# Decoder stack: the first two row tiles of the expert stage prepared inside the gated attention

## The chip, the cores and the metric

The kernel runs on one core of a Trainium2 chip. The metric is the device time of one execution in microseconds (us): the median over runs of the same program. A profile is one further execution, recorded instruction by instruction, with a time of its own. The engines are named as in the profile: PE is TensorE (PEld its weight loads), DVE VectorE, ACT ScalarE, POOL GpSimd, SP SyncE, which only issues DMAs here.

## The reference

The input x has 16 blocks of 128 tokens with 512 features, in f32. Six sublayers follow each other, each as `x = layernorm(x + sublayer(x))`: a state-space scan, a cross attention, a ternary feed-forward, a self attention, a gated cross attention, and a mixture of experts. The change touches the last two.

Gated attention (16 heads of 32), per batch of 128 tokens against 128 context tokens: `out = softmax(q k^T) v @ wo.T`, then `sigmoid(x @ wg.T) * out`, where x is the RMS-normed input.

Experts: a router scores 64 experts and keeps the 8 best; the 64 lie in 8 groups of 8. For each group g a token has `scalar` (the sum of its kept weights in that group) and `soft` (the softmax over the kept ones):

```python
xg = x[:, None, :] + jnp.einsum('ngi,ghi->ngh', soft, mask_up_w)
g = jnp.einsum('ngh,gih->ngi', xg, gate_proj_w)
u = jnp.einsum('ngh,gih->ngi', xg, up_proj_w)
d = jnp.einsum('ngi,ghi->ngh', silu(g) * u, down_proj_w)
y = jnp.einsum('ng,ngh->nh', scalar, d)
```

A group in which a token has nothing (scalar 0) adds nothing for it, so only the tokens of a group need be computed.

## The kernel before, in words

The stages run in the order of the sublayers: scan, cross attention, feed-forward, then `stage_attention`, which holds both the self attention (8 pairs of blocks) and the gated attention (8 pairs), and `stage_moe`. The x blocks stay in SBUF throughout.

**Gated attention.** `stage_attention` has a list `units` of 16 pairs x 8 = 128 entries, and a loop over steps t from -2 to 129. In step t, unit t gets its exponentials on ACT (`exps`, L1184), unit t-1 its row sums and scaling (`norm`: DVE L1190 and L1191, POOL L1192), unit t-2 its transpose on TensorE (`pts`, copied to `at_T` by ACT L1028 or DVE L1030; the PSUM tile of it has one buffer). Side jobs are Python generators in a list `running`; each gets one `next` per step. `project` makes q and the gates of a pair ahead of its units; `values`, started when half a pair is turned, multiplies with v (`ao`), copies (`oT`), multiplies with wo (`pw`, L1214), gates on DVE (L1217) and adds to x on POOL (L1218), and after the second half normalises the pair. After the loop, a `while running` drains what is left. The last pair's attention ends with a `pw`, a gate and an add.

**Routing.** From step 84 on, an object `Moe` lives in `k.moe`. Its `setup` loads the router, the weights of expert group 0 (`first`) and, by `prepare`, the mask table `mup[0]`. `tick` runs `route` for a pair of finished blocks: it transposes x, scores, chooses, and forms rows of 776 numbers per token: 512 of x, 4 x 64 of group softmax (a high and a low part), 8 of `scalar`. `scatter` writes each row to DRAM (`rows`), and by indirect DMA on POOL's queue (L1492) to the next free place in `bucket[half][g]` of every group that the token uses. Blocks 0 to 7 are the first half, and are routed while the gated attention works on blocks 8 to 15; blocks 8 to 15 are routed from step 3 of the expert loop on.

**Experts.** `stage_moe` walks `units` of (half, group, tile): 128 rows each, 6 tiles for a bucket of 768 rows, 8 for the last group of the second half, 98 in all. It is a software pipeline over steps t, in which a unit passes through
- `fetch` (L1502, SP): 128 rows, 388 KB, from the bucket into tile `row`, 6 buffers, 5 steps ahead;
- `places` (L1507, L1509), 3 ahead: TensorE turns the 128 softmax columns (`pts`), ACT copies them to `soft`;
- `masks` (L1513, L1515), 2 ahead: TensorE multiplies with `mup` (`pm`), DVE adds x (`xg`);
- `turn_in` (L375, L1521), 1 ahead: four transposes (`ptx`), copied by ACT to `xgT`;
- `gate_up` (L1529 to L1533): 4 chunks of `pg` and `pu`, each recorded as two matmuls, Silu on ACT, product with `scalar` on DVE into `act`; `pg` and `pu` have one PSUM buffer each;
- `turn_act` (L1539), `down` (L1546, `y`), `store` (L1556, and a DMA on ACT's queue), one and two steps later.

`load` fetches the 2.1 MB of weights of the next group on SP, `prepare` casts its mask table (ACT L1368, three DVE operations), `combine` gathers results by indirect DMA on POOL's queue and adds them to x there.

**Memory.** Pools are opened and closed like a stack, from two sides. The attention's work pool `s4w` is on the left; the router's `s6r`, in `k.moe_ctx`, is on the right and stays to the end. When `stage_attention` returns, its pools close, and `stage_moe` opens `s6w` (row, soft, xg, xgT, act and so on), `s6m` (weights) and `s6u` (mask tables) in their place. In PSUM the attention has `s4p` (tag `pp`, two buffers), `s4s`, `s4t`, `s4o`; the experts have `s6g` (pg, pu), `s6p` (tag `pp`, three buffers), `s6k` (pm), `s6y`.

**Order.** The language's framework places the waits and orders the instructions of each engine by itself: the order in which the program writes them is their rank, and one of lower rank goes ahead where its own estimate of durations says that the one of higher rank isn't ready. Each engine then works its queue in that order. So the order of the trace isn't always that of the program: `turn_in` of unit 1 is written ahead of `gate_up` of unit 0, and stands behind its first two pairs in the trace.

## Time and profile before

| | us |
|---|---|
| median of 3 runs | 3377.56 (3376.58 to 3380.5) |
| profiled execution | 3382.4 |
| its span, first to last instruction | 3380.6 |
| PE busy | 3153.0 (93%) |
| DVE, POOL, ACT busy | 1876.7, 1389.5, 1379.5 |
| last matmul of the attention (pw) starts, group lasts | 2480.81, 3.70 |
| first matmul of the experts (pts) starts | 2489.80 |
| first gate_up matmul (pg) starts | 2494.01 |
| last y group starts, lasts | 3364.12, 5.32 |

The expert stage thus takes about the last 890 us of the span. The profile tells, for each stretch of time, how long each engine was busy and at which granted clock TensorE ran (1.00 is full); for each instruction, its start, its duration, and in square brackets how long its engine was idle before it and what ended that; and for each wait, its engine and line, what it waited for, the total, how often and the longest. In the timeline, neighbouring instructions of a kind are merged (x8), and matmuls overlap, so starts are to be compared with starts. A group of `pg` and `pu` matmuls that runs freely starts every 0.59 us for two of them; the ends of matmuls are modelled.

### The profile page before, as it was taken

To read this page: it belongs to the slowest core of one execution; us is meant where nothing else is said; L and a number is where in the kernel's file an instruction comes from. 1 tells how busy PE (TensorE), PEld (TensorE's weight loads), DVE (VectorE), ACT (ScalarE), POOL (GpSimd) and SP (SyncE) were. 2 spreads that over 40 slices of the span, in tenths; PEclk is the share of its full clock that TensorE was granted. 3 is DMA by queue.
4 is the path that set the end of the run, shared out by engine and by line. 5 is a ranking of instruction groups with operands and counts; after the bars stand their busy time and mean duration, and the time that the engine had idled before them with its cause. 6 is when DMAs were issued, how large, how long until landed. Compare 5 with 4: busy or idle time off the path is not lost. (4 is left out here: it accounts for less than half of the span.)

```text
span 3380.6 us, 38522 instructions
## 1 busy us (share of the span) xinstructions
PE 3153.0 (93%) x12894; PEld 1813.6 (54%) x12944; DVE 1876.7 (56%) x4202; ACT 1379.5 (41%) x3299; POOL 1389.5 (41%) x1198
## 2 busy tenths in 40 slices
PE   6888999899999999999799989998989999989998
PEld 3444444355555555555466555665655566556665
DVE  5877888456556556455576669765643232222223
ACT  4655655133333233234333379865643232112221
POOL 6967887133323333332000066325624454233331
PEclk8999999899999999999899989999999999999999
DMA  6887332200000000002200010013335665445441
GB/s 230 261 259 223 98 88 69 68 7 4 7 4 4 7 4 4 7 1 94 91 1 1 17 47 1 11 57 148 137 133 175 201 233 189 163 156 172 163 158 65
DMA packets 161553, 317.28 MB, mean 94 GB/s; under 512 B 19113, under 2 KB 82089, under 8 KB 158276
## 3 DMA queue, kind: packets, MB, share of 16 engines
q1 hardware_dynamic: 123012, 215.83, 20.8%
q0 software_dynamic: 19328, 64.56, 5.5%
q10 hardware_dynamic: 19008, 34.35, 2.7%
q8 instruction: 105, 1.72, 0.2%
q14 instruction: 100, 0.82, 0.1%
HBM read 238.80 MB, written 129.04 MB: 109 GB/s over the span
## 5 line engine op out<-in xcount | busy, mean ns | idle before, releaser
L245 POOL TENSOR_TENSOR dBx<-dtx,BC 128x1024 f32<-128x1024 f32 x128 | 301.2, 2373 | 44.8 <-DVE h L258 35.1
L1529 PE MATMUL pg<-gu,xgT 128*128 128x352 f32 x784 | 301.7, 467 | 0.0
L1529 PE MATMUL pu<-gu,xgT 128*128 128x352 f32 x784 | 299.6, 464 | 0.0
L1546 PE MATMUL y<-dn,aT 128*128 128x512 f32 x588 | 268.3, 592 | 0.0
L1533 DVE SCALAR_TENSOR_TENSOR act<-pu,row,act 128x352 f32<-128x352 f32 x98 | 57.1, 583 | 376.3 <-PE pu L1529 317.9
L575 POOL TENSOR_TENSOR pr<-pr,sm 128x512 f32<-128x512 f32 x128 | 134.7, 1053 | 289.6 <-DVE sm L574 244.2
L236 ACT ACTIVATE h<-dt,negA 128x254 f32<-128x254 f32 x512 | 239.8, 474 | 14.9 <-DVE dt L178 2.1
L1572 POOL TENSOR_TENSOR x<-got,x 128x512 f32<-128x512 f32 x120 | 152.2, 1274 | 226.4 <-DMA got<-results,gidx 225.2
L606 PE MATMUL po<-w,aT 128*128 128x512 f32 x512 | 232.2, 597 | 1.1 <-DVE aT L600 1.1
L483 PE MATMUL pq<-w,xT 128*128 128x512 f32 x512 | 228.9, 594 | 0.0
L1565 POOL DMA_INDIRECT got<-results,gidx x120 | 116.2, 968 | 268.9 <-DMA results<-yo 216.1
L460 POOL TENSOR_TENSOR m<-m,m 128x512 f32<-128x512 f32 x96 | 121.6, 1267 | 247.0 <-DVE m L455 247.0
L258 DVE TENSOR_TENSOR_SCAN h<-h,dBx 128x1024 f32<-128x1024 f32 x80 | 183.0, 2294 | 71.0 <-ACT h L236 48.7
L568 ACT ACTIVATE pr<-sc,mx,sf 128x256 f32<-128x256 f32 x256 | 142.8, 562 | 187.0 <-DVE mx L561 176.1
L267 PE MATMUL py<-hC,ident 128*128 128x512 f32 x320 | 164.6, 643 | 49.1 <-ACT y L272 49.1
L1529 PEld LDWEIGHTS pu<-gu,xgT 128*128 128x128 f32 x784 | 151.2, 193 | 85.1 <-issue 4.2
L1529 PEld LDWEIGHTS pg<-gu,xgT 128*128 128x128 f32 x784 | 144.1, 194 | 64.7 <-issue 3.0
L1532 ACT ACTIVATE act<-pg 128x352 f32<-128x352 f32 x98 | 45.5, 464 | 318.6 <-PE pg L1529 248.9
L1546 PEld LDWEIGHTS y<-dn,aT 128*128 128x128 f32 x588 | 104.1, 190 | 100.8 <-issue 94.2
L1521 ACT COPY xgT<-ptx 128x512 f32<-128x512 f32 x98 | 57.5, 587 | 233.9 <-PE ptx L375 209.6
L483 PEld LDWEIGHTS pq<-w,xT 128*128 128x128 f32 x512 | 93.5, 190 | 102.0 <-issue 99.0
L606 PEld LDWEIGHTS po<-w,aT 128*128 128x128 f32 x512 | 95.4, 191 | 96.9 <-issue 92.9
(363 smaller groups left out, 6808.3 us busy)
## 6 DMA issues: line engine op xcount, KB each, us to landing
bucket<-zeros SPq DMA_DIRECT2D x96, 388.0 KB
row<-bucket SPq DMA_DIRECT2D x90, 388.0 KB
BC<-bcd SPq DMA_DIRECT2D x128, 256.0 KB
results<-yo ACTq DMA_DIRECT2D x90, 256.0 KB
gu<-in_moe_guT SPq DMA_DIRECT2D x16, 1408.0 KB
cT<-in_ctxT SPq DMA_DIRECT2D x32, 256.0 KB
dn<-in_moe_downT SPq DMA_DIRECT2D x16, 512.0 KB
rows<-r_row SPq DMA_DIRECT2D x16, 388.0 KB
```

What stands on the lines that cost most here:

```text
L236: nc.scalar.activation(h[:, c, :, 1:], st.dt[:, c].rearrange("p (b t) -> p b t", b=BQ)[:, :, 1:], AF.Exp, scale=negA[:, c, n : n + 1])
L245: nc.gpsimd.tensor_tensor(dBx, st.dtx, BC[:, 0].unsqueeze(1).to_broadcast([P, KC, TQ]), ALU.mult)
L258: nc.vector.tensor_tensor_scan(hf, hf, df, 0.0, ALU.mult, ALU.add)
L267: nc.tensor.matmul(st.py[c], k.ident, st.hC[n][:, 2 * c : 2 * c + 2], start=n == 0, stop=n == NS - 1)
L460: nc.gpsimd.tensor_tensor(m1, m1, m2, ALU.add)
L483: nc.tensor.matmul(ps, src[:, c], w[c], start=c == 0, stop=c == KC - 1)
L568: nc.scalar.activation(pr[:, j], st.sc[g, i][:, j], AF.Exp, scale=st.sf[:, h : h + 1], bias=st.mx[g, i][:, j : j + 1], accum_out=sm[:, j : ...
L575: nc.gpsimd.tensor_tensor(pr, pr, sm.unsqueeze(2).to_broadcast([P, 2, 2 * P]), ALU.mult)
L606: nc.tensor.matmul(st.po, aT[:, j], k.wo[h // 8][:, h % 8], start=h == 0, stop=h == G * J - 1)
L1529: nc.tensor.matmul(ps, u.xT[:, c], gu[:, c, lo : lo + I], start=c == 0, stop=c == KC - 1)
L1546: self.nc.tensor.matmul(u.y, u.aT[:, c], u.w[1][:, c], start=c == 0, stop=c == 2)
L1572: nc.gpsimd.tensor_tensor(k.x[b], got, k.x[b], ALU.add)
```

## The change

A new generator `open` makes a small pool `s6o` on the right side, in `k.moe_ctx`, and there the tiles row, soft, xg and xgT of two units, which are the first two tiles of `bucket[0][0]`. It is put into `running` at step len(units)-8 = 120 of the attention's loop, so its first step runs in step 121: the two row DMAs. Two steps later it does `places` for the first and the second unit, then `masks` for each, then `turn_in` for each, one per step. `masks` takes its PSUM tile from the attention's `pp` buffers there. `stage_moe` uses these two units for its first two, leaves out their fetch, places, masks and turn_in, and starts its loop at t = -3 in place of -5. Everything else of the two units (`act` and after) still lives in `s6w`, as do the rows of units 2 and up. The pool of 15.4 KB per partition stays open to the end.

```diff
@@ -1286,6 +1286,9 @@
             if k.moe:
                 k.moe.tick()
                 k.moe.send()
+            if t == len(units) - 8:
+                assert not (k.moe.now or k.moe.sending or k.to_route)
+                running.append(k.moe.open())
         while running:
             k.moe.tick()
             for job in list(running):
@@ -1498,8 +1501,24 @@
 
 
     def fetch(self, u):
-        u.row = self.wk.tile([P, self.ROW], F32, tag="row", name="row", bufs=6)
+        u.row = self.wk.tile([P, self.ROW], F32, tag="row", name="row", bufs=self.depth)
         self.nc.sync.dma_start(u.row, u.src)
+
+    def open(self):
+
+        self.wk = self.k.moe_ctx.enter_context(self.k.tc.tile_pool(name="s6o", bufs=2, side="right"))
+        self.pm, self.depth, self.opened = self.pp, 2, []
+        for j in range(2):
+            u = Ctx()
+            u.g, u.src = 0, self.k.bucket[0][0][j * P : (j + 1) * P, :]
+            self.opened.append(u)
+            self.fetch(u)
+        yield
+        yield
+        for link in (self.places, self.masks, self.turn_in):
+            for u in self.opened:
+                link(u)
+                yield
 
     def places(self, u):
         at = D + P * (u.g // 4)
@@ -1509,7 +1528,7 @@
         self.nc.scalar.copy(u.soft, pt)
 
     def masks(self, u):
-        pm = self.pm.tile([P, D], F32, tag="pm", name="pm")
+        pm = self.pm.tile([P, D], F32, tag="pp" if self.pm is self.pp else "pm", name="pm")
         self.nc.tensor.matmul(pm, u.soft, self.mup[u.g], start=True, stop=True)
         u.xg = self.wk.tile([P, D], F32, tag="xg", name="xg")
         self.nc.vector.tensor_tensor(u.xg, pm, u.row[:, 0:D], ALU.add)
@@ -1588,7 +1607,7 @@
     nc, tc, m = k.nc, k.tc, k.moe
     NG, T, H = m.NG, m.TILES, NB // 2
     with ExitStack() as ctx:
-        m.wk = wk = ctx.enter_context(tc.tile_pool(name="s6w", bufs=2))
+        m.wk, m.depth = ctx.enter_context(tc.tile_pool(name="s6w", bufs=2)), 6
         wp = ctx.enter_context(tc.tile_pool(name="s6m", bufs=2))
         mp = ctx.enter_context(tc.tile_pool(name="s6u", bufs=1))
         m.pgu = ctx.enter_context(tc.tile_pool(name="s6g", bufs=1, space=PSUM))
@@ -1600,7 +1619,7 @@
             for g in range(NG):
                 last = h and g == NG - 1
                 for j in range(H if last else T):
-                    u = Ctx()
+                    u = Ctx() if len(units) >= len(m.opened) else m.opened[len(units)]
                     u.h, u.g, u.j, u.b = h, g, j, H + j
                     u.src, u.to = (k.rows[u.b][:, :], None) if last else (
                         k.bucket[h][g][j * P : (j + 1) * P, :], k.results[h][g][1 + j * P : 1 + (j + 1) * P, :]
@@ -1613,7 +1632,7 @@
                 if next(job, running) is running:
                     running.remove(job)
 
-        for t in range(-5, len(units) + 4):
+        for t in range(-3, len(units) + 4):
             if t == 3:
                 k.to_route += range(H // 2, H)
             m.tick()
@@ -1626,6 +1645,8 @@
                 if not 0 <= t - lag < len(units):
                     continue
                 u = units[t - lag]
+                if u in m.opened and what in (m.fetch, m.places, m.masks, m.turn_in):
+                    continue
                 if what == m.fetch:
                     u.w = None
                 if what == m.gate_up:
```

## The prediction

> **What bounds the kernel now.** I read the page's engine totals and slices first (TensorE 93% busy, 9 tenths in almost every slice of the expert stage), then stretches of 15 us around the hand-over from attention to experts, then the waits of TensorE there, then the order of single instructions. Stretches (columns: bounds, length, busy time and count of PE, PEld, DVE, ACT, POOL; granted clock; DMA share; GB/s):

> ```profile
> 2455.00:2470.00 15.00, 14.14 (x105) 8.16 (x104) 9.05 (x25) 13.60 (x55) 7.51 (x7) 1.00 0.01 2
> 2470.00:2485.00 15.00, 11.58 (x96) 5.94 (x96) 7.94 (x25) 3.91 (x12) 4.58 (x4) 1.00 0.01 1
> 2485.00:2500.00 15.00, 9.20 (x25) 5.74 (x26) 5.29 (x18) 3.25 (x6) 1.26 (x1) 0.66 0.84 281
> 2500.00:2515.00 15.00, 15.00 (x62) 9.78 (x61) 5.48 (x9) 4.58 (x11) 0.00 (x0) 1.00 0.73 249
> ```

> TensorE is full before 2470 and after 2500; in between it is partly empty, and from 2485 to 2500 what it does runs at a clock of 0.66. The waits of TensorE (2440 to 2520) name the cause, and its timeline gives the places:

> ```profile
> PE pts L1507 <- DMA row<-bucket: 5.3, 1, 5.3
> PE ao L1204 <- ACT at_T L1028: 0.7, 1, 0.7
> PE pw L1214 <- ACT oT L1210: 0.7, 1, 0.7
> ```

> ```profile
> 2480.81 3.70 PE L1214 MATMUL pw<-x_wo,oT 128*128 128x512 f32 x8 [0.70 <-ACT oT L1210]
> 2489.80 0.45 PE L1507 MATMUL pts<-ident,row 128*128 128x128 f32 x1 [5.29 <-DMA row<-bucket]
> 2490.64 0.79 PE L1513 MATMUL pm<-mup,soft 128*128 128x512 f32 x1 [0.40 <-ACT soft L1509]
> ...
> 2494.01 1.54 PE L1529 MATMUL pg<-gu,xgT 128*128 128x352 f32 x2
> 2495.35 1.38 PE L1529 MATMUL pu<-gu,xgT 128*128 128x352 f32 x2
> 2496.52 1.06 PE L375 MATMUL ptx<-ident,xg 128*128 128x128 f32 x4
> ...
> 2506.87 0.49 PE L1539 MATMUL pta<-ident,act 128*128 128x128 f32 x3
> ```

> The last attention product ends at 2484.51. The first expert product starts at 2494.01, behind a DMA, a transpose, the mask product and a second transpose. Why the DMA is so late is told by SyncE and GpSimd:

> ```profile
> 2432.98 0.32 SPq L1099 DMA_DIRECT2D v<-x_v  x1
> 2486.61 1.27 SPq L1502 DMA_DIRECT2D row<-bucket  x3
> 2487.92 0.43 SPq L1381 DMA_DIRECT2D gu<-in_moe_guT  x1
> ```

> ```profile
> 2485.32 1.26 POOL L1218 TENSOR_TENSOR x<-x,gate 128x512 f32<-128x512 f32 x1 [5.65 <-DVE gate L1217]
> ```

> SyncE had nothing to do for 53 us; the rows go out 0.03 us after the last reader of attention's work pool (2485.32+1.26 = 2486.58). It is the room, not the data, that holds them. Call this release R.

> **What the stretch is worth.** My mark is 2506.87, where gate_up of units 0 and 1 is done. From 2484.51 to it are 22.36 us. At the full clock the work in it is: gate_up twice, 16 matmuls at the 0.296 us spacing of the timeline after 2504 = 4.73 each, 9.46; 4 pts at 0.11, 3 pm at 0.32, 3 ptx at 0.44 (from start to the next start, after 2504); together 12.2. So 10.2 us are lost: 5.29 waiting for the row, 0.97 for soft and xg, some 3.9 to the low clock and the act handshake (pg and pu have one buffer each).

> **The change, part by part.** Moved, for each of two units: one 388 KB row DMA on SyncE, one pts (0.11) and its soft copy (ACT 0.27), one pm (0.32) and its add (DVE 0.69), four ptx matmuls (0.44 together) and the xgT copy (ACT 0.59). In all: two DMAs, TensorE 1.74 us, ACT 1.72, DVE 1.38; nothing on GpSimd.

> The two DMAs. SyncE's queue is empty from 2433.3 to 2486.6, so nothing stands behind them. They need the last scatter into the first bucket, issued at 2430.09 by GpSimd; an indirect transfer elsewhere in the trace is used 3.7 us after issue (got, 2520.47, added at 2524.15). Landed well before 2450, and places comes at step 123, near 2459. Cost nothing; were they held until 2459, a landing of 3.2 us (2486.61 to 2489.80) would hold TensorE in attention for that long.

> The tail of attention. ACT is 13.60 of 15 us busy until the last exponentials (2471.5), then nearly idle. DVE has no gap from 2471.56 to 2478.3, where it carries a layernorm and two at_T copies for which pts waits. TensorE idles 0.86+1.41+0.73+0.70 = 3.70 us between 2469 and 2481. If all moved work falls into idle time, the tail grows by nothing; if none does, by TensorE's 1.74. An add of 0.69 that lands in DVE's full stretch is late at at_T, then at the last ao and pw. I take 1.0, a little over half.

> What it opens. Once xgT of unit 1 is copied, gate_up(0) has its inputs. pg and pu lie in s6g, which is opened first as s4p was, so I take its room as free when the last s4p tile is read, which is that copy. No row shows this. Early end: gate_up(0) puts 1.43 us into the gaps at 2479 and 2480.8 and finishes 3.30 us after the last pw, at 2487.8. Late end: it starts at R, ends at 2491.3. In both, act(0) needs the new pool and so R, a Silu of 0.46 and a DVE multiply of 0.58: gate_up(1) starts 0.6 us later, loses another 0.7 on pu, and takes 4.73. Then pts, pm and ptx of unit 2 and a pts of unit 3 add 0.98. The mark is at 2487.8+0.6+0.7+4.73+0.98 = 2494.8 early, 2498.3 late; with the 1.0 of the tail 2495.8 and 2499.3. Saved: 11.1 or 7.6. I take the early end, since the pool that is replaced is read no later than that.

> Rows 2 and 3. Row 2 is now first at R and lands at 2489.8 plus the tail, while gate_up(0) and (1) cover it. Before row 3 stand row 2, gu and dn: 388+1408+768+388 = 2952 KB at the 346 GB/s of 2488 to 2500 is 8.5 us from 2487.5, 2496 to 2497. It is needed for gate_up(3), about 2506: covered, if its pts is not queued ahead of gate_up(1).

> The mask table of expert 1 and the following ones are cast on ACT behind their own loads; those loads do not move, while the units come 9 us sooner. In the profile such casts kept ACT waiting 0.33, 2.23, 3.40 and 2.11 us, mean 2.0, hidden then by a TensorE that was late itself. I charge one: 2.0. Both bounds: nothing, or 8 for all four.

> **The clock rule.** The row: granted clock 0.50 from 2488 to 2498 after an idle 5.29 us. [...]

> **Sum.** 11.1 - 2.0 = 9.1 us. All of the expert stage hangs on TensorE after this and routing starts by unit count, so the shift reaches the end. In the profiled execution (3382.4, span 3380.6) that makes 3373.3; it lay 4.8 above the median of 3377.56, from which I forecast 3368.5.

> **Rivals.** (a) Same queue, same wait: pts of unit 2 stands ahead of gate_up(0) in TensorE's order. Then gate_up(0) starts after row 2 (2489.8+1.0+0.45 = 2491.2 instead of 2494.0), as cold as before: 2.8, and 0.9 for the transposes gone: 3374. Against it: the order seen before is not the written one (ptx of unit 1 stands behind two pairs of gate_up(0)), so what is ready goes first. (b) A wait replaces a wait: pts of unit 3 or the casts stop TensorE or ACT up to 2497; 4 to 6 left, 3372.5. (c) Slower: the order is planned anew from step 121 on, and ACT's queue has a trap:

> ```profile
> 2590.16 0.62 ACT L1459 COPY r_row<-x 128x512 f32<-128x512 f32 x1 [9.65 <-DMA bucket<-r_row,r_to]
> 2592.50 1.08 PE L375 MATMUL ptx<-ident,xg 128*128 128x128 f32 x4 [4.47 <-DVE xg L1515]
> ```

> A copy of routed rows waits for the scatter, Silu waits behind it, TensorE stops for 4.47 us and restarts cold (2592.5 to 2597, 2.4 more): 7. Two such stops are in the trace (the other is 5.58). If the new order puts more of those copies ahead of Silu, each that is over 6 us early costs 7; three more make +21-9 = 12, 3389; at two it is already over the line, 3382. (d) That the tiles are not early at all is excluded: nothing holds them.

> **Chances.** Forecast 0.55, (a) 0.15, (b) 0.12, (c) 0.18. A measurement of this kernel tells about 0.2%, 6.8 us, from no change: faster below 3370.8. (a) and (b) fall within it. The forecast's own range is 3364 to 3371; 3362 to 3384 takes in (a), (b) and the nearer half of (c).

> **What would show it.** Right: row DMAs on SyncE near 2435 to 2460; pts, pm, ptx of two units among attention's; the first pg before or just after the last pw; no TensorE wait over 3 us between 2480 and 2500 and a clock near 1.0 there; pta of unit 0 about 2496. Wrong: the last pw more than 2 us later; pts of unit 2 ahead of the first pg with a wait of 5 us; more than two stops on r_row behind 2550.

## The result and the profile after

The changed kernel takes 3372.56 us (median of 22 runs, 3366.25 to 3381.15), the kernel before 3379.55 (22 runs, 3376.52 to 3384.7): a ratio of 0.998 with a 95% interval of 0.9973 to 0.9986. The forecast was 3368.5. The change helps, by 7.0 us where 9.1 were forecast; that is hardly more than the 0.2% that can be told from no change, and the interval (4.7 to 9.1 us) doesn't by itself part the two. The profiled execution of the changed kernel has a span of 3373.5 us, 7.1 under the 3380.6 of before.

The four stretches of 15 us around the hand-over, same columns as before (bounds, length, busy time and count of PE, PEld, DVE, ACT, POOL; granted clock; DMA share; GB/s):

```profile
2455.00:2470.00 15.00, 15.00 (x104) 8.63 (x103) 8.05 (x21) 11.12 (x46) 7.51 (x7) 0.91 0.01 2
2470.00:2485.00 15.00, 14.45 (x115) 8.64 (x114) 9.36 (x27) 5.83 (x17) 4.59 (x4) 1.00 0.00 1
2485.00:2500.00 15.00, 12.10 (x38) 6.86 (x36) 6.12 (x19) 3.34 (x7) 1.27 (x1) 0.89 0.73 265
2500.00:2515.00 15.00, 14.09 (x56) 8.88 (x56) 5.59 (x10) 4.67 (x11) 0.32 (x1) 1.00 0.74 272
```

TensorE is now 14.45 us busy from 2470 to 2485 (before 11.58), and 12.10 from 2485 to 2500 (before 9.20). Two things are not as forecast: it is not full behind the attention, and its clock is still below 1.00 there (0.89 from 2485 to 2500). The waits of TensorE from 2440 to 2520 say what is left (those of the hand-over; one of 2.5 us ahead of it is in both profiles):

```profile
PE pts L1526 <- DMA row<-bucket: 1.7, 3, 0.7
PE pg L1548 <- ACT act L1551: 1.4, 1, 1.4
PE ptx L375 <- DVE xg L1534: 0.5, 1, 0.5
PE pu L1548 <- DVE act L1552: 0.2, 1, 0.2
```

The one wait of 5.3 us for a row has become three with 1.7 together, and one of 1.4 on ACT is new. TensorE's timeline gives the places (start, duration, engine, line, tiles; idle time before it and its end in brackets):

```profile
2463.39 0.27 PE L1526 MATMUL pts<-ident,row 128*128 128x128 f32 x1
...
2478.95 0.76 PE L1548 MATMUL pg<-gu,xgT 128*128 128x352 f32 x2
...
2482.53 3.60 PE L1214 MATMUL pw<-x_wo,oT 128*128 128x512 f32 x8
...
2487.74 0.76 PE L1548 MATMUL pu<-gu,xgT 128*128 128x352 f32 x2
2489.86 0.86 PE L1548 MATMUL pg<-gu,xgT 128*128 128x352 f32 x2 [1.37 <-ACT act L1551]
2491.47 0.30 PE L1526 MATMUL pts<-ident,row 128*128 128x128 f32 x1 [0.75 <-DMA row<-bucket]
2491.98 1.54 PE L1548 MATMUL pu<-gu,xgT 128*128 128x352 f32 x2 [0.21 <-DVE act L1552]
...
2498.77 0.33 PE L1526 MATMUL pts<-ident,row 128*128 128x128 f32 x1 [0.57 <-DMA row<-bucket]
...
2499.37 0.49 PE L1558 MATMUL pta<-ident,act 128*128 128x128 f32 x3
...
2501.93 0.66 PE L375 MATMUL ptx<-ident,xg 128*128 128x128 f32 x4 [0.50 <-DVE xg L1534]
...
2507.23 2.74 PE L1565 MATMUL y<-dn,aT 128*128 128x512 f32 x6
```

The first product of the experts starts at 2478.95, ahead of the attention's last; half of unit 0's `gate_up` lies before 2482.53. Then come three stops, and after them a group of two `pg` or `pu` matmuls takes 1.17 us to the next start (2493.74, 2494.91) instead of 0.59: the clock is at 0.50 (from 2491.82 to 2495.23). SyncE, GpSimd and ACT at the same place:

```profile
2430.97 0.87 SPq L1505 DMA_DIRECT2D row<-bucket  x2
...
2488.23 0.32 SPq L1505 DMA_DIRECT2D row<-bucket  x1
2488.60 0.43 SPq L1384 DMA_DIRECT2D gu<-in_moe_guT  x1
```

```profile
2486.93 1.27 POOL L1218 TENSOR_TENSOR x<-x,gate 128x512 f32<-128x512 f32 x1 [6.18 <-DVE gate L1217]
```

```profile
2488.05 1.28 ACT L1551 ACT_TABLE_LOAD   x1 [6.08 <-PE pg L1548]
2489.34 0.46 ACT L1551 ACTIVATE act<-pg 128x352 f32<-128x352 f32 x1
```

The first two rows left at 2430.97, and nothing waited for them. The release R (end of the last POOL add) is at 2488.20, and row 2 goes out 0.03 us behind it. Between the end of `pg` of unit 0 and its Silu stands a load of ACT's function table, 1.28 us; without it the Silu could have started at R, 1.1 us sooner. The kernel before had the load too, but ahead of the end of `pg`, which the Silu then waited for:

```profile
2498.22 1.28 ACT L1532 ACT_TABLE_LOAD   x1
2500.96 0.47 ACT L1532 ACTIVATE act<-pg 128x352 f32<-128x352 f32 x1 [1.46 <-PE pg L1529]
```

**The yardstick.** Runs of one kernel differ by some us ahead of the hand-over: the fourth `pw` group from the attention's end took 3.70 us in the profile of before and 5.82 in that of after, where the clock was at 0.50 for 10.2 us ahead of it and through most of it (2447.45 to 2457.69), against 3.4 us in the profile of before (2450.44 to 2453.85). That isn't the change's doing: warm_three, which has the kernel before up to there, shows 5.83. So I count from the `pts` that starts at its end (2458.20 before, 2459.05 after). From there (the two runs of 4057.68 us in table_rows and 3434.13 in all_rows, at mean granted clocks of 0.748 and 0.924 where the others have 0.96 to 0.97, are left out of all ratios and medians here):

| run | last pw ends | first y starts | ratio to before, 95% interval |
|---|---|---|---|
| before | 26.31 | 55.19 | |
| changed | 27.08 | 48.18 | 0.9980 (0.9973 to 0.9986) |
| again (the same) | 27.08 | 48.08 | 0.9979 (0.9969 to 0.9989) |
| rows_only | 26.32 | 52.13 | 0.9993 (0.9984 to 1.0002) |
| one_tile | 27.67 | 51.67 | 0.9989 (0.9982 to 0.9995) |
| warm_before | 26.30 | 56.94 | 1.0006 (0.9998 to 1.0014) |
| warm_three | 26.31 | 55.53 | 1.0006 (0.9999 to 1.0012) |
| table_early | 27.06 | 48.30 | 0.9979 (0.9971 to 0.9987) |
| rows_first | 27.07 | 46.07 | 0.9975 (0.9965 to 0.9985) |
| norm_late | 27.08 | 48.04 | 0.9977 (0.9967 to 0.9987) |
| table_rows | 27.07 | 43.01 | 0.9967 (0.9955 to 0.9980) |
| table_rows_2 | 27.08 | 43.30 | 0.9959 (0.9947 to 0.9971) |
| all_rows | 27.07 | 42.62 | 0.9961 (0.9948 to 0.9974) |
| all_rows_2 | 27.08 | 42.78 | 0.9964 (0.9952 to 0.9977) |

The first `y` is 7.01 us earlier in the changed kernel. The `y` groups keep that lead up to 2579 and gain about 1.0 on it by the end, at the waits near 2590, 2940 and 2975; less the 0.85 by which the anchor is later, the span is 7.1 shorter. The column of the first `y` repeats within 0.3 us for the three kernels that were profiled twice (the kernel before has one profile only), so it tells more than the totals, whose intervals are some 0.2% wide.

### The profile page after: what moved, and what is told of

Read it like the earlier page. It is cut to its first block, busy times and chain, and to the rows that moved or that the text cites. A ratio compares the mean times of both kernels' runs of the same rounds, so it can differ in the third digit from the quotient of the medians.

```text
span 3373.5 us, 38567 instructions
## 1 busy us (share of the span) xinstructions
PE 3163.2 (94%) x12944; PEld 1816.9 (54%) x12944; DVE 1871.9 (55%) x4202; ACT 1379.4 (41%) x3299; POOL 1390.2 (41%) x1198
## 3 DMA queue, kind: packets, MB, share of 16 engines
q1 hardware_dynamic: 123012, 215.83, 20.7%
q8 instruction: 105, 1.72, 0.2%
## 5 line engine op out<-in xcount | busy, mean ns | idle before, releaser
L267 PE MATMUL py<-hC,ident 128*128 128x512 f32 x320 | 166.4, 649 | 48.2 <-ACT y L272 47.1
```

The lines of the kernel that those rows point to most:

```text
L267: nc.tensor.matmul(st.py[c], k.ident, st.hC[n][:, 2 * c : 2 * c + 2], start=n == 0, stop=n == NS - 1)
```

## The experiments

**rows_only: the DMAs alone.** Only the two row DMAs are moved by the program; places, masks and turn_in stay in the expert loop.

```diff
     def open(self):
...
             self.fetch(u)
         yield
-        yield
-        for link in (self.places, self.masks, self.turn_in):
-            for u in self.opened:
-                link(u)
-                yield
...
-                if u in m.opened and what in (m.fetch, m.places, m.masks, m.turn_in):
+                if u in m.opened and what == m.fetch:
```

> The changed kernel with only the two row DMAs in open(); places, masks and turn_in of the two units stay in the expert stage. My theory (row wait, fill chain and low clock are three separate parts of the gain): the 5.3 us wait for the row becomes a wait for the release of the work pool only, some 2 to 2.6 us, TensorE stays at the full clock, but the chain soft-pm-xg-ptx-xgT stands where it stood; 3.5 to 5.5 us faster than before, so some 2 to 3 slower than the changed kernel. Rival (the late DMA is the whole matter): 7 faster than before, level with the changed kernel. Rival (only an early gate_up helps): under 2 faster than before.

Measured: first y 3.06 us earlier than before, a little under the 3.5 to 5.5 expected, and the clock does not stay at 1.00; ratio 0.9993, an interval that takes in 1. Its timeline of TensorE behind the attention's last product, which ends at 2480.88:

```profile
2483.30 0.50 PE L1527 MATMUL pm<-mup,soft 128*128 128x512 f32 x1 [2.42 <-ACT soft L1523]
...
2486.38 1.54 PE L1543 MATMUL pg<-gu,xgT 128*128 128x352 f32 x2 [0.25 <-ACT xgT L1535]
```

The early DMAs of the two rows are worth 3.06 of the 7.01. Both `pts` went early with them, into the attention (2469.82), but `soft` has its tile in the released room: ACT starts it at 2482.98, 0.03 us behind the last POOL add, and TensorE stops 2.42 us for it in place of the row. The clock falls all the same: it is at 0.50 from 2484 to 2490. The other 3.95 come from having the mask products and the second transposes done, and with them a `gate_up` ready to fill the gap; these parts were not separated.

**one_tile: one unit instead of two.**

```diff
-        for j in range(2):
+        for j in range(1):
...
-        for t in range(-3, len(units) + 4):
+        for t in range(-4, len(units) + 4):
```

> The changed kernel with one unit opened in place of two; the second is fetched, masked and turned in the expert stage. My theory: gate_up of unit 0 fills TensorE up to about 3 us behind the last pw as in the changed kernel, but unit 1 has its row only 3.2 us after the release and its xgT some 4 us later, so gate_up of unit 1 starts about 2495 in place of 2490 to 2492: 3 to 4.5 us slower than the changed kernel, 2.5 to 4 faster than before. Rival (gate_up of unit 1 waits for act of unit 0 anyway, so the second tile buys nothing): level with the changed kernel within 1 us.

Measured: first y 3.52 us earlier than before, ratio 0.9989. TensorE runs out of work behind `gate_up` of unit 0 and waits for the row of unit 1:

```profile
2488.54 0.76 PE L1548 MATMUL pu<-gu,xgT 128*128 128x352 f32 x2
2493.38 0.45 PE L1526 MATMUL pts<-ident,row 128*128 128x128 f32 x1 [4.08 <-DMA row<-bucket]
```

So the second tile is worth 3.5 us: it is the cover for the fetch of the next row, as the forecast had it.

**warm_before: what the fallen clock cost before.** The kernel before, with six 128x512 products that nobody reads behind the last POOL add (warm_three, below, has three).

```diff
+        if i == 1 and self.b0 == NB - 2:
+            fill = self.pp.tile([P, D], F32, tag="pp", name="fill")
+            for _ in range(6):
+                nc.tensor.matmul(fill, self.xs[i][:, 0:P], self.xs[i], start=True, stop=True)
```

> The kernel before with six idle 128x512 matmuls put behind the last POOL add of the attention (their result is not used), from about 2486.7 to 2489.3, so that TensorE idles 2.1 us and not 5.3 ahead of the first pts. [...] Rival (the gain of the change is mostly the clock): 5 us or more faster. [...]

Measured: first y 1.75 us later, ratio 1.0006.

```profile
2490.41 7.12 PE L1223 MATMUL fill<-x 128*128 128x512 f32 x12 [2.12 <-POOL x L1218]
2497.36 0.38 PE L1511 MATMUL pts<-ident,row 128*128 128x128 f32 x2
```

The filler was too long: each product makes two records, and they hold the first `pts` until 35.38 behind the anchor instead of 31.60. But from that `pts` to the first `y` it takes 21.56 us instead of 23.59: 2.0 less. All of that stretch ran at 1.00; the low clock had come and gone under the fillers, between 2490 and 2496 (same columns as above):

```profile
2490.00:2492.00 2.00, 1.59 (x3) 0.80 (x4) 1.44 (x6) 0.00 (x0) 0.35 (x1) 0.85 0.35 50
2492.00:2494.00 2.00, 2.00 (x4) 0.76 (x3) 1.72 (x9) 0.00 (x0) 0.00 (x0) 0.50 0.96 346
2496.00:2498.00 2.00, 1.74 (x6) 0.66 (x4) 0.44 (x1) 0.21 (x2) 0.00 (x0) 1.00 1.02 370
```

From the first `pts` to the first `y` both kernels do the same 81 matmuls. Before, they kept TensorE busy for 22.59 us at a mean clock of 0.82; here for 19.41 at 1.00. So the low clock had drawn the work out by 3.2 us. At the full clock TensorE waits 1.15 us more (2.15 against 1.00, for `soft`, `xg` and `xgT`), which leaves the 2.0.

**table_early: the new wait on ACT.** The changed kernel, with the table of Silu loaded at the end of the attention, behind the last exponentials.

```diff
+        tc.keep_in_program_order(nc.scalar.preload_act_table_set("silu_and_others"))
```

> The changed kernel with the Silu table loaded on ACT behind the last oT copy, and not between pg of unit 0 and its Silu, where it takes 1.28 us while TensorE waits 1.37 us for act. My theory: Silu starts at the release (2488.2), 1.1 us sooner, and the DVE multiply moves ahead of the layernorm's small operations, which is worth up to 1.5 more; 1 to 2.5 us faster than the changed kernel, 8 to 9.5 faster than before. Rival (rows 2 to 4 set the pace by then): the 1 to 2 us turn up again as a longer wait of pts for its row, level with the changed kernel within 0.5.

Measured: first y 0.12 us later than in the changed kernel, ratio 0.9979. The load is gone from the path, and yet nothing is won, as the rival had it:

```profile
2490.78 1.45 PE L1549 MATMUL pg<-gu,xgT 128*128 128x352 f32 x4 [0.26 <-ACT act L1552]
2492.44 1.45 PE L1549 MATMUL pu<-gu,xgT 128*128 128x352 f32 x4 [0.20 <-DVE act L1553]
...
2500.62 0.40 PE L1527 MATMUL pts<-ident,row 128*128 128x128 f32 x1 [4.00 <-DMA row<-bucket]
```

The waits of unit 1 shrink from 1.37, 0.75 and 0.21 to 0.26 and 0.20. The edit does more than move the load: with it the framework also puts unit 0's multiply ahead of the layernorm's small operations (1.56 us behind R instead of 3.14), and `pts` of unit 2 behind eight matmuls of unit 1 instead of two, which covers row 2. Then `pts` of unit 3 waits 4.00 us for its row. Row 3 is landed 10.4 us after R here (2490.2 to 2500.6), and 10.6 in the changed kernel (2488.20 to 2498.77): it stands in SP's queue behind the weights of group 1, and what TensorE does earlier doesn't hasten it. The forecast had seen that row at 2496 to 2497, needed near 2506. It is needed much sooner, because its `pts` stands ahead of `pta` of unit 0 in TensorE's order: this is the mechanism of rival (b).

**rows_first: the row chain alone.** The load of group 1's weights moves from step -2 to step 2 of the expert loop.

```diff
-            n = t + 8
+            n = T if t == 2 else 0 if t == T - 8 else t + 8
             if n % T == 0 and n // T < 2 * NG and n // T not in weights:
                 weights[n // T] = m.load(wp, n // T % NG)
+            n = t + 8
             if n % T == 0 and 0 < n // T < NG:
```

> The changed kernel, but the weights of group 1 are loaded four steps later, so that the row fetches of units 3 to 7 stand ahead of them in SP's queue. Theory (rows of units 3 and on arrive late because they stand behind the weight transfers): the waits of 0.57 and 0.41 us of pts on its row go, and the first y matmul starts 1 to 2 us earlier than in the changed kernel; total 1 to 2 us less. Rival (the table load and the multiply of unit 0 set the pace alone): first y within 0.5 us of the changed kernel's, the total within 1 us of it.

Measured: first y 2.11 us earlier than in the changed kernel, ratio 0.9975 (the total alone can't tell it from the changed kernel). Of the waits on rows only the first is left:

```profile
PE pg L1548 <- ACT act L1551: 1.4, 1, 1.4
PE pts L1526 <- DMA row<-bucket: 0.8, 1, 0.8
```

The waits of units 3 and 4 are gone, and the 0.5 for `xg` behind them. The theory is right, and its upper end was a little low. The table load, row 2 and the fallen clock stay (1.4 us for `act`, 0.8 for the row, 0.50 from 2492 to 2494).

**table_rows: both.** The two edits above together.

> The changed kernel with the Silu table loaded at the end of the attention and with the row fetches ahead of the weights of group 1. Theory (each of the two hides the other: the table alone only moved the wait to row 3, where it was 4.0 us): the wait of 4.0 us goes, the TensorE clock stays up behind it, first y starts 4 to 5.5 us earlier than in the changed kernel (about 43 us behind the anchor instead of 48.2), and the total is 4 to 5.5 us less, 11 to 12.5 us under the kernel before. Rival (row 2, fetched in the released space, or the weights of group 1, take the wait over): first y within 1 us of the changed kernel's and no gain in the total.

Measured: first y at 43.01, 5.17 us earlier than in the changed kernel and 12.18 earlier than before; median 3366.97 against 3379.7, ratio 0.9967. Its TensorE behind the attention:

```profile
2488.27 1.45 PE L1549 MATMUL pg<-gu,xgT 128*128 128x352 f32 x4 [0.26 <-ACT act L1552]
2489.92 1.45 PE L1549 MATMUL pu<-gu,xgT 128*128 128x352 f32 x4 [0.20 <-DVE act L1553]
2491.21 0.27 PE L1527 MATMUL pts<-ident,row 128*128 128x128 f32 x1
```

No row is waited for: `pts` of unit 2 stands behind eight matmuls of unit 1, as in table_early, and they cover its row. Stretches of 2 us, the changed kernel first, then this one (the granted clock is the third number from the end):

```profile
2490.00:2492.00 2.00, 1.04 (x4) 0.32 (x4) 1.59 (x8) 0.20 (x1) 0.00 (x0) 0.95 1.02 404
2492.00:2494.00 2.00, 2.00 (x4) 1.40 (x5) 1.02 (x3) 0.07 (x1) 0.00 (x0) 0.50 1.02 390
2494.00:2496.00 2.00, 2.00 (x6) 1.17 (x6) 0.67 (x1) 0.00 (x0) 0.00 (x0) 0.69 1.07 398
```

```profile
2490.00:2492.00 2.00, 2.00 (x8) 1.20 (x9) 1.72 (x10) 0.27 (x1) 0.00 (x0) 1.00 1.08 367
2492.00:2494.00 2.00, 2.00 (x12) 1.45 (x12) 1.46 (x4) 1.21 (x3) 0.00 (x0) 1.00 0.95 351
2494.00:2496.00 2.00, 1.93 (x10) 1.04 (x8) 1.93 (x4) 1.36 (x4) 0.00 (x0) 1.00 1.01 391
```

The theory's numbers hold (43 behind the anchor, 4 to 5.5 us). The table alone gave -0.12, the rows alone 2.11, both 5.17. Up to the `pts` of unit 3 the changed kernel has two chains side by side: TensorE's own (the table load, row 2, the multiply, the low clock), and row 3's way through the queue, 10.6 us behind R. TensorE comes to that `pts` only 0.57 us ahead of the row, so each chain hides the other; with both gone the clock stays at 1.00. What the load, the multiply and the new order are worth one by one was not separated.

**all_rows: what is left besides.** table_rows, and the last pair's layernorm on VectorE moved behind unit 0's multiply, and `act` of the two early units in their own pool, so that unit 0's Silu need not wait for R.

```diff
+        if i == 1 and self.b0 == NB - 2:
+            return
...
-        u.act = self.wk.tile([P, I], F32, tag="act", name="act")
+        u.act = (self.own if u in self.opened else self.wk).tile([P, I], F32, tag="act", name="act")
...
+                layernorm(k, k.x[NB - 2 :], k.x[NB - 2 :], pin=tc.keep_in_program_order)
```

> As the run with table and rows, and also the last pair's layernorm on VectorE behind the multiply of unit 0, and the activation buffers of the two early units in their own pool. Theory (the multiply of unit 0 waited about 1.5 us behind the layernorm's small operations): 1 to 2 us less than the run with table and rows. Rival (row 2, which lands about 3 us behind the release, ends last): within 0.7 us of that run.

Measured: first y 0.39 us earlier than in table_rows, ratio 0.9961. The rival is right. `pg` of unit 1 follows without a wait, and what then stops TensorE is row 2:

```profile
PE pts L1529 <- DMA row<-bucket: 0.4, 1, 0.4
```

**norm_late: the layernorm alone.** The changed kernel with only the layernorm edit of all_rows.

> The changed kernel with the last pair's layernorm on VectorE moved behind the multiply of unit 0. Theory A (the waits add up: the multiply stood 1.5 us behind the layernorm, so that is lost time): first y 1.0 to 1.5 us earlier than in the changed kernel, 18.1 to 18.6 after the end of its last pw group less 1.5, that is about 19.6 to 20.1 us behind that end instead of 21.1. Theory B (pts of unit 2 stands ahead of the second pair of unit 1 in TensorE's order and its row lands only about 3 us after the release, so the multiply is hidden behind the row): first y within 0.4 us of the changed kernel's, 20.7 to 21.5 us behind the end of the last pw group.

Measured: first y at 48.04, 20.96 us behind the end of the last `pw`, against 21.10 in the changed kernel (21.00 in its second profile). Theory B is right. Unit 0's multiply starts 3.7 us behind the last `pw`'s end instead of 5.2. Row 2 holds its `pts` as before (5.32 us behind that end, 5.34 in the changed kernel). The `pu` behind it is 0.39 sooner, and that is lost at the `pts` of unit 3, which waits 0.82 for its row:

```profile
2490.47 0.33 PE L1528 MATMUL pts<-ident,row 128*128 128x128 f32 x1 [0.74 <-DMA row<-bucket]
2490.61 1.36 PE L1550 MATMUL pu<-gu,xgT 128*128 128x352 f32 x2
```

The 1.5 us by which the layernorm holds up the multiply are covered by the rows.

**warm_three: three fillers, ending near the row.** warm_before with `range(3)`.

> The kernel before with three added 128x512 matmuls of float32 (result unused) in the gap between the attention and the first expert unit, where six had delayed the first transpose by about 4 us. Theory (the fallen clock behind the gap costs about 2 us, and three fillers end near the landing of the row): first transpose delayed by at most 1 us, first y 1 to 2 us earlier than in the kernel before, total 1 to 2 us less. Rival (the first idle stretch of about 2 us ahead of the fillers lowers the clock already, and three fillers don't bring it back): first y 0 to 1 us later than before, total the same or up to 1 us more.

Measured: first y 0.34 us later than before, ratio 1.0006. The rival is right. The first `pts` is 1.2 us later than before, a little more than the 1 us expected, because the fillers themselves ran slow (a granted clock of 0.68 from 2486 to 2488, 0.50 from 2488 to 2490):

```profile
2485.77 4.54 PE L1223 MATMUL fill<-x 128*128 128x512 f32 x6 [2.12 <-POOL x L1218]
```

Six records in 4.54 us; behind them the clock rises (0.97 from 2490 to 2492), then falls again to 0.50 from 2494 to 2496, after waits of 0.48, 0.68 and 0.33 us. Filling the gap paid in neither run (0.34 and 1.75 us later).

**again, table_rows_2, all_rows_2: on one chip beside the changed kernel.**

> The changed kernel itself, for a comparison on one chip with the three runs beside it. Every theory expects what it gave: a ratio to the kernel before between 0.997 and 0.999, some 7 us less.

> The run with table and rows once more, beside the changed kernel on one chip. Theory (5.2 us of its hand-over are gone): 4 to 6.5 us under the changed kernel of this call, ratio to before 0.996 to 0.9973. Rival (the gain of the first look was luck of the chip): within 2 us of the changed kernel.

> The run with all parts once more, beside the changed kernel on one chip. From its first look: first y 0.4 us earlier than in the run with table and rows, so a total within 1 us of that run, and 4.5 to 7 us under the changed kernel.

Measured: 3376.41 us (again), 3367.89 (table_rows_2) and 3368.98 (all_rows_2), with 3381.18 for the kernel before beside them. table_rows_2 is 8.5 us under the changed kernel by the medians and 6.8 by the ratios (0.9979 - 0.9959 = 0.0020 of 3381), the first more and the second slightly more than expected; the hand-over itself is worth 4.8 of it (first y 48.08 against 43.30). all_rows_2 is 7.4 under the changed kernel by the medians and 5.1 by the ratios; its first y is 0.52 earlier than that of table_rows_2, its total 1.1 us longer, which these runs can't tell apart. The version to keep is table_rows: two edits of a line or two on top of the change, about 12 us under the kernel before (12.7 and 13.3 by the medians beside the two, 11.2 and 13.9 by the ratios).

## Why the prediction was right, and where it was not

The sign and the mechanism held: it was room, not data, that held the rows, and an early start of the two tiles is worth their wait. The time, 3372.56, lies above the forecast's own range (3364 to 3371) and within the wider one. By its own steps:

- **The two DMAs at nothing: right.** They left at 2430.97, used first at 2463.39.
- **The tail at 1.0: right, slightly less.** The last `pw` ends at 27.08 instead of 26.31, 0.77.
- **The early end of `gate_up(0)`: right, and better.** 8 of its 16 matmuls lie before the attention's last product; it is done at 2488.33 (2487.74 and two spacings of 0.296), 2.2 us behind the end of the last `pw` (2486.13), where 3.30 were forecast.
- **From there to the mark: wrong.** The sum had 0.6 + 0.7 + 4.73 + 0.98 = 7.0 us; it took 11.0 (2488.33 to 2499.37). The 4.0 are three terms. *"needs the new pool and so R, a Silu of 0.46"* left out the table load ahead of that Silu: `pg` of unit 1 came 1.53 behind instead of 0.6 (0.9). The 0.7 on `pu` became 1.53 (2490.45 to 2491.98; 0.8), for row 2, which was to be covered, was not: its `pts` stands ahead of that `pu`. The last 0.2 of it is DVE's multiply, behind the layernorm. And the rest of unit 1 took 7.39 instead of 5.12 (2.3): 0.57 waiting for row 3, the remaining 1.7 the clock, which was at 0.50 for 3.4 us of it with TensorE busy for 3.25. With 1.1 gained on `gate_up(0)` and 0.2 on the tail, the mark is saved 8.35 us, 2.75 under the early end's 11.1.
- **Rows 2 and 3 covered: wrong.** Row 3 landed near 2498.7 where 2496 to 2497 was forecast, and was needed ahead of the mark, not near 2506. The step itself named the condition ("if its pts is not queued ahead"); table_early showed that this row alone sets the pace when the rest is faster. After the mark TensorE stood 0.41 for row 4 and 0.50 for `xg`; from start to start these two cost 1.3, and the lead of 8.35 fell to 7.01.
- **The charge of 2.0 for the casts: hardly spent.** The first cast of the next mask table (2499.41) follows its predecessor without a wait, and TensorE waits for no cast. But the two DVE operations behind that cast (2500.06 and 2500.79) stand ahead of `xg` (2501.19), whose `pm` was done at 2500.1: the 0.50 on `xg` is theirs. The later casts cost nothing that shows, for the lead stays the same up to 2579. The two mistakes had opposite signs, which is luck: without this charge the forecast would have been 11.1, and missed by 4.1 instead of 2.1.
- **The clock: the sum was made at the full one.** It was at 0.50 from 2491.82 to 2495.23 and cost the 1.7 above. As for its price in the kernel before, the forecast read 3.9 us for the low clock and the handshake together. warm_before says 3.2 in drawn-out work, 2.0 after the waits that came back; in the profile of before the clock was at 0.50 for 10.2 us (2487.98 to 2498.22).
- **"The shift reaches the end": right.** Rival (c) did not come about: the stops on `r_row` are as many as before. The second holds TensorE for 5.42 us (5.58 before). The first, 6.6 us earlier and no longer:

```profile
2583.57 0.62 ACT L1462 COPY r_row<-x 128x512 f32<-128x512 f32 x1 [9.18 <-DMA bucket<-r_row,r_to]
2585.91 1.08 PE L375 MATMUL ptx<-ident,xg 128*128 128x128 f32 x4 [4.00 <-DVE xg L1534]
```

- **Rival (a): refuted.** `pts` of unit 2 stands behind all of `gate_up(0)`. **Rival (b)** was part of the truth: its mechanism took about 2.2 us of waiting (0.75 for row 2, 0.57 and 0.41 for rows 3 and 4, 0.50 for `xg`), and its time, 3372.5, is what was measured. That is partly chance: of the 4.1 us between forecast and median, 2.1 are the sum's, and 2.0 come from the kernel before, whose median over 22 runs is 3379.55 and not the 3377.56 of three.

That the three terms together cost what they are said to is shown as follows: with the table early and the rows first, the mark (`pta` at 2494.51) is 35.93 behind the anchor instead of 48.67, saved 12.7 us, more than the early end promised. The size of the clock's 1.7 is read from the trace; as a cause it was not separated from the waits that come before it, for no run had the one without the other.

## What to carry to other kernels

Before counting on an instruction to start early, list everything that stands ahead of it on its own engine, loads of function tables included: a cost hidden by the old wait comes into the open with it (here a load of 1.28 us). When a wait is removed, work out two next ones, not one; where two chains of nearly equal length lie side by side, shortening one shows nothing (-0.1 us) or a part (2.1), and shortening both 5.2, so an edit that fails alone is not refuted. And let the order of a DMA queue follow need: rows that are needed in 4 us belong ahead of weights needed much later (rows_first: 2.11 us).

## What the runs showed of the hardware that was not expected

TensorE's busy time in 4 us around the hand-over, and the granted clock in the 2 us behind them:

| profile, stretch | TensorE busy, of 4 us | clock in the next 2 us |
|---|---|---|
| before, 2484 to 2488 | 0.51 | 0.50 |
| table_early, 2496 to 2500 | 0.62 | 0.69, then 0.50 |
| rows_only, 2480 to 2484 | 1.38 | 0.50 |
| changed, 2488 to 2492 | 1.67 | 0.50 |
| rows_first, 2488 to 2492 | 1.68 | 0.50 |
| warm_three, 2490 to 2494 | 2.52 | 0.50 |
| changed, 2498 to 2502 | 2.52 | 1.00 |
| before, 2478 to 2482 | 2.56 | 1.00 |
| warm_before, 2482 to 2486 | 2.57 | 1.00 |
| table_rows, 2488 to 2492 | 3.54 | 1.00 |

2.52 us of work stand ahead of 0.50 in warm_three (where the clock was 0.89 in the second half of the stretch) and ahead of 1.00 in the changed kernel, so the amount alone doesn't tell it. What does was not shown.

Nor do the traces show what brings it back. In the profile of before it was at 0.50 from 2487.98 to 2498.22, with TensorE busy for 7.42 of these 10.2 us; in the changed kernel for 3.4 us, 3.25 of them busy. Ahead of the anchor, from 2449 to 2457 in the changed kernel, it was at 0.50 with TensorE busy throughout. There one and the same wait of 2.5 us stands at the start of a low spell of 3.4 us in the profile of before and of 10.2 in that of the changed kernel, and the same work from its end to the anchor took 7.93 and 10.88 us.

Products put into a gap behind 2.1 us of waiting ran slow themselves (warm_three: 6 records in 4.54 us, at 0.68 and then 0.50, against 3.60 for the eight of a `pw` group at 1.00), so those fillers paid the low clock that they were to prevent.
